# A graph network of four layers: 768 columns of its second adjacency sweep behind the attention sweep and at two levels

## Chip, core and metric

The kernel runs on one core of a Trainium2 chip, in float32. The time is what the device takes for one execution of the whole program, in microseconds (us). A core has a matrix engine (TensorE, PE in the profile; PEld is its weight loading), a vector engine (VectorE, DVE), a scalar engine (ScalarE, ACT) and GpSimd (POOL). SyncE (SP), ACT and POOL issue DMA transfers. Each engine works through its own list of instructions in order, and waits in front of one until what it needs is there.

## What is computed

`adj` is a sparse 2708 x 2708 matrix held dense, `x` has 2708 rows of 512 features. Four layers follow one another, each a residual and a layer normalisation:

```python
deg = maximum((adj != 0).sum(-1), 1)
# layer 0
inc = adj + mask / norm(mask)                     # mask = adj > 0, by row
x = LN(x + (inc @ x) / inc.sum(-1))
# layer 1
ts = adj @ x
gate_a, gate_b = sigmoid([ts, x] @ Wa.T + ba), sigmoid([ts, x] @ Wb.T + bb)
e = where(adj != 0, exp(-leaky_relu(x @ W_sa @ a_l + (x @ W_sa @ a_r).T)), 0)
x_a = (e / (e.sum(1) + 1e-5)) @ (x @ W_sa)
x_b = adj @ (x @ W_gcn) + b_gcn
x = LN(x + sigmoid(gate_a * x_a + gate_b * x_b))
# layer 2: p = adj @ p three times, out = x @ w0 + p1 @ w1 + p2 @ w2 + p3 @ w3
x = LN(x + out)
# layer 3
x = LN(x + relu(((adj + I) scaled by deg on both sides @ x + x) @ W_out + b_out))
```

So there are seven products of a 2708 x 2708 matrix with a 2708 x 512 one: one for layer 0, two for layer 1 (`adj @ x`, from which both the gates and x_b are made, and the attention product), three hops for layer 2 (the product by a weight is folded in after Horner, so that the innermost factor is x @ w3, called Y0) and one for layer 3.

## The kernel before

**Tiling.** The matrix is taken transposed (`adjT`), in four quarters of 1354 x 1354 (NH), called 11, 12, 21, 22. The inner dimension runs in ten tiles of 128 rows (KW) and 74 leftover rows (KR), which are done apart (`rest`). The free dimension, "columns" here, belongs to the rows of the result. X is held in SBUF as blocks B11, B12, B21, B22 with the sums T1 to T4, in groups A to D of three k tiles (B and D hold two each, and have a spare third part, `spare_part`, in which weights and score vectors are kept).

**One-level sweep** (`sweep`, line 374). A product is made from quarters by the scheme of Winograd, with seven products in place of eight, PLAIN giving their order. It takes its columns in ranges, RANGES on line 30: 384, 384, 256, 330. In a range each of the seven products has ten k tiles and two halves of the features, 140 matmuls. `load` brings the tiles of adjT on SP's queue; `comb` (line 400) makes the sums s1 to s4 of the quarters on DVE, ahead of the product that reads them. In the second sweep `comb` also stores each sum to DRAM (SD, shown as As), on POOL's queue, for the later sweeps.

**Two-level sweep** (`sweep2`, line 1181). The scheme is applied twice, 49 products in place of 64. RANGES2 (line 42) has two groups, 338 and 339 columns wide, each holding two such strips of each half. ORDER2 gives the order of the seven outer products. In each, `load` brings four strips of five k tiles (K2) from adjT or from the stored sums; `comb` (line 1212) makes inner sums of strips on DVE, `tsum` (line 1246) those of X; `step` (line 1267) multiplies; `leave` (line 1291) and `add` (line 1303) combine the outer products on DVE. The hops have a sixth k tile (ext), which multiplies X2 (the result of layer 1, stored transposed as X2T) by a weight, with its own quarter sums (`ext_loads`, `ext_sums`, SE).

**Stages.** `S = 28 s` gives stage s a place of 28 units. Work is put at a position by `at(pos, fn)`; the list is sorted by position, and a scheduler takes the order within each engine from it, freely from position 5 (START) on. A call with `hold=True` pins its instructions behind the one before on the same engine. Stages: S[0] layer 0, S[1] `adj @ x` of layer 1, S[2] the attention product, S[3] to S[5] the hops, S[6] layer 3. A one-level range has 7 units, a group of the two-level sweep 14.

**Around S[1].** `spread_v` (line 891) writes the four score vectors over the partitions. `score` (line 904) multiplies a tile of X1 by each of them on DVE, eight operations a tile of 128 rows, placed 0.95 units apart; `scores_end`, `score_rows`, `scores_over` turn them into `s_left`, `s_right` and `gate_x`. `tally` (line 965) counts the entries of a column tile by tile on DVE (`deg`). `done1` (line 996) makes the gates, and for the first three ranges x_b with the seven-product form (`row_sums`, `seven`, lines 624 and 638), for the last with `dense` (line 600). What it stores is XB.

**S[2].** `prep2` (line 1061) makes the attention weights of a tile: two ACT activations (lines 1066, 1067) and one DVE operation (line 1068), in place of the tile `a` of adjT. `done2` (line 1088) multiplies by W_sa, adds XB, applies the sigmoid and the layer normalisation (`layernorm`, line 553; its power is a POOL instruction on line 560), transposes X2 and makes Y0 with `dense`.

## Time and profile before

| | us |
|---|---|
| median of 3 runs | 2887.13 |
| their lowest and highest | 2880.56, 2888.68 |
| the profiled execution | 2883.33 |
| its span, first to last instruction | 2881.2 |
| PE busy in it | 2832.7 |
| DVE busy in it | 2195.9 |

The page adds up what each engine was busy with. The windows view does so for stretches of the span, in columns for PE, PEld, DVE, ACT and POOL, with the granted clock of PE, the mean busy share of the 16 DMA engines and GB/s. The timeline gives start, duration and name of merged records. The view of waits gives what an engine stood still for. A line of a group ends with its count, its busy time, the mean of one in ns, and the idle time before it with what ended it:

```profile
L1212 DVE TENSOR_TENSOR z<-z 128x339 f32<-128x339 f32 (+1 forms) x966 | 454.3, 503 | 12.5 <-PE accu L1267 3.2
L403 DVE TENSOR_TENSOR a<-a,a 128x384 f32<-128x384 f32 (+2 forms) x330 | 162.4, 510 | 23.1 <-PE accu L458 22.4
L965 DVE SCALAR_TENSOR_TENSOR deg<-a,deg 128x384 f32<-128x384 f32 (+2 forms) x152 | 75.2, 505 | 19.0 <-DMA a<-in_adjT 17.9
```

In the trace the second sweep starts at about 431 us, the attention sweep at about 830, the first hop at 1366, and layer 3 at 2482 us of the span.

### The profile page before, as it was taken

To read this page: it belongs to the slowest core of one execution; us is meant where nothing else is said; L and a number is where in the kernel's file an instruction comes from. 1 tells how busy PE (TensorE), PEld (TensorE's weight loads), DVE (VectorE), ACT (ScalarE), POOL (GpSimd) and SP (SyncE) were. 2 spreads that over 40 slices of the span, in tenths; PEclk is the share of its full clock that TensorE was granted. 3 is DMA by queue.
4 is the path that set the end of the run, shared out by engine and by line. 5 is a ranking of instruction groups with operands and counts; after the bars stand their busy time and mean duration, and the time that the engine had idled before them with its cause. 6 is when DMAs were issued, how large, how long until landed. Compare 5 with 4: busy or idle time off the path is not lost. (4 is left out here: it accounts for less than half of the span.)

```text
span 2881.2 us, 37482 instructions
## 1 busy us (share of the span) xinstructions
PE 2832.7 (98%) x10963; PEld 1870.3 (65%) x10963; DVE 2195.9 (76%) x5670; ACT 550.1 (19%) x1119; POOL 617.6 (21%) x1113
## 2 busy tenths in 40 slices
PE   7999999999999999999999999999999999999998
PEld 5655665657765656866666666666666666666665
DVE  6898798576736464654699787887878877799987
ACT  4544200111136444542100000000000100100001
POOL 0123223123320101122203123031230211501202
PEclk9999999999999999999999999999999999999999
DMA  7665466354544333565667767566675666754542
GB/s 229 193 212 179 133 204 218 124 181 143 183 140 130 117 113 98 151 198 151 195 205 236 213 192 246 166 201 208 187 250 168 181 197 182 230 174 145 175 142 92
DMA packets 368524, 510.04 MB, mean 177 GB/s; under 512 B 63424, under 2 KB 321700, under 8 KB 368320
## 3 DMA queue, kind: packets, MB, share of 16 engines
q1 hardware_dynamic: 302392, 370.56, 43.5%
q0 software_dynamic: 49344, 126.38, 13.1%
q10 hardware_dynamic: 16584, 10.71, 1.3%
q8 instruction: 87, 1.43, 0.2%
q14 instruction: 117, 0.96, 0.1%
HBM read 423.77 MB, written 83.65 MB: 176 GB/s over the span
## 5 line engine op out<-in xcount | busy, mean ns | idle before, releaser
L1212 DVE TENSOR_TENSOR z<-z 128x339 f32<-128x339 f32 (+1 forms) x966 | 454.3, 503 | 12.5 <-PE accu L1267 3.2
L1285 ACT COPY q<-accu 128x338 f32<-128x338 f32 (+1 forms) x84 | 34.6, 443 | 1003.3 <-PE accu L1267 806.0
L560 POOL TENSOR_TENSOR rstd<-rstd,neg_half 128x1 f32<-128x1 f32 (+3 forms) x91 | 59.3, 652 | 762.2 <-DVE rstd L559 516.6
L1267 PE MATMUL accc<-s,t 128*128 128x338 f32 (+1 forms) x644 | 198.1, 450 | 0.0
L1267 PE MATMUL accu<-z,t 128*128 128x338 f32 (+1 forms) x644 | 194.0, 448 | 1.5 <-DVE z L1212 1.5
L1267 PE MATMUL accd<-z,t 128*128 128x338 f32 (+1 forms) x644 | 193.9, 448 | 0.6 <-DVE q L1349 0.6
L1267 PE MATMUL accc<-z,t 128*128 128x338 f32 (+1 forms) x644 | 193.5, 448 | 0.5 <-ACT q L1285 0.5
L1400 POOL DMA_DIRECT2D Y<-y x192 | 105.1, 554 | 366.3 <-DVE y L1395 333.3
L403 DVE TENSOR_TENSOR a<-a,a 128x384 f32<-128x384 f32 (+2 forms) x330 | 162.4, 510 | 23.1 <-PE accu L458 22.4
L1267 PEld LDWEIGHTS accc<-s,t 128*128 128x128 f32 x644 | 120.9, 190 | 64.1 <-issue 7.5
L1267 PEld LDWEIGHTS accc<-z,t 128*128 128x128 f32 x644 | 122.0, 190 | 61.6 <-issue 1.0
L1267 PEld LDWEIGHTS accu<-z,t 128*128 128x128 f32 x644 | 121.7, 190 | 61.7 <-DVE z L1212 2.0
L1267 PEld LDWEIGHTS accd<-z,t 128*128 128x128 f32 x644 | 121.9, 190 | 60.5 <-DVE q L1349 1.5
L1212 DVE TENSOR_TENSOR s<-z 128x338 f32<-128x338 f32 (+1 forms) x322 | 149.7, 503 | 12.7 <-PE accc L1267 8.4
L1291 DVE TENSOR_TENSOR q<-q,accd 128x338 f32<-128x338 f32 (+1 forms) x112 | 56.0, 500 | 115.2 <-PE accd L1267 115.2
L1068 DVE SCALAR_TENSOR_TENSOR a<-a,e 128x384 f32<-128x384 f32 (+2 forms) x160 | 77.4, 507 | 49.8 <-ACT e L1067 49.5
L1066 ACT ACTIVATE e<-row,s_right 128x384 f32<-128x384 f32 (+5 forms) x176 | 96.3, 569 | 76.2 <-PE accc L458 20.4
L965 DVE SCALAR_TENSOR_TENSOR deg<-a,deg 128x384 f32<-128x384 f32 (+2 forms) x152 | 75.2, 505 | 19.0 <-DMA a<-in_adjT 17.9
L406 POOL DMA_DIRECT2D As<-a x120 | 64.9, 544 | 82.3 <-DVE a L403 80.3
L1067 ACT ACTIVATE e<-e 128x384 f32<-128x384 f32 (+5 forms) x176 | 79.3, 477 | 1.8
L606 PE MATMUL ps_d<-w,xT 128*128 128x512 f32 (+1 forms) x176 | 79.2, 593 | 0.4 <-ACT xT L597 0.4
L769 DVE SCALAR_TENSOR_TENSOR s<-a,row 128x384 f32<-128x384 f32 (+2 forms) x152 | 75.0, 505 | 6.0 <-ACT row L754 6.0
(683 smaller groups left out, 5869.0 us busy)
## 6 DMA issues: line engine op xcount, KB each, us to landing
z<-As SPq DMA_DIRECT2D x320, 169.5 KB
z<-As SPq DMA_DIRECT2D x320, 169.0 KB
a<-in_adjT SPq DMA_DIRECT2D x240, 192.0 KB
z<-in_adjT SPq DMA_DIRECT2D x240, 169.5 KB
z<-in_adjT SPq DMA_DIRECT2D x240, 169.0 KB
a<-in_adjT SPq DMA_DIRECT2D x120, 165.0 KB
a<-in_adjT SPq DMA_DIRECT2D x112, 128.0 KB
As<-a POOLq DMA_DIRECT2D x60, 192.0 KB, 4.2
```

The source lines that it names most:

```text
L403: nc.vector.tensor_tensor(A[r, dst, k][:, :n], A[r, a, k][:, :n], A[r, b, k][:, :n], op)
L406: nc.gpsimd.dma_start(out=SD[m][k * P : (k + 1) * P, R0 : R0 + n], in_=A[r, dst, k][:, :n])
L560: nc.gpsimd.tensor_tensor(rstd[:w, 1:2], rstd[:w, 0:1], neg_half[:w], ALU.pow)
L606: nc.tensor.matmul(o, lhs(c), r, start=c == 0 and n == 0, stop=c == DC - 1, skip_group_check=True)
L769: nc.vector.scalar_tensor_tensor(t[:w, :n], a[:w, :n], 0.0, row[R0, h][:w, :n], ALU.is_gt, ALU.mult)
L965: nc.vector.scalar_tensor_tensor(d[:w, :n], a[:w, :n], 0.0, d[:w, :n], ALU.not_equal, ALU.add)
L1066: nc.scalar.activation(e[:w, :n], row[R0, h][:w, :n], AF.Prelu, bias=s_right[:w, t : t + 1], alpha=0.01)
L1067: nc.scalar.activation(e[:w, :n], e[:w, :n], AF.Exp, scale=-1.0)
L1068: nc.vector.scalar_tensor_tensor(a[:w, :n], a[:w, :n], 0.0, e[:w, :n], ALU.not_equal, ALU.mult)
L1212: nc.vector.tensor_tensor(d[:, :n], Z[x + (k,)][:, :n], Z[y + (k,)][:, :n], op)
L1267: nc.tensor.matmul(B[home][:, :n], stat(v, k), a[:, :n], start=bool(start and k == 0), stop=k == nk - 1, skip_group_check=True)
L1400: nc.gpsimd.dma_start(out=rows[:, :, f * P : (f + 1) * P], in_=o[32 * f : 32 * (f + 1), : m * P].rearrange("p (b d) -> p b d", d=P))
```

## The change

The second sweep (S[1]) keeps only the columns from 768 on (RANGES_A) and takes 14 units in place of 28. Columns 0 to 767 are done in a new stage B at position 70, between the attention sweep and the first hop, as one group of the two-level sweep with strips of 384 columns (RANGES_B). For that the groups of all two-level sweeps become 293 and 384 wide.

The sums of quarters for those columns, which the sweep made on its way, are made in S[2] by a background task of its own: for each of two strips of 384 columns and each of ten k tiles four tiles are loaded on POOL's queue into six buffers (the four weight buffers `w_0` to `w_3` and two of the pool `nat`), counted (`back_tally`), summed (`back_sums`) and stored. The tallies and sums are held. The score sums of all tiles come within S[1]; those for the gates of columns below 768 come in S[2] with a second fetch of X1. `done2` leaves x_a of these columns, without gate, in XB. `doneB` makes gates, x_b with `dense`, X2 and Y0 for them; Y0 of the others follows in stage B from X2T. `W[3]` is loaded there. Positions of some loads in `next_x2` move with it.

```diff
-RANGES2 = [(0, 338), (676, 339)]
+RANGES_A = [(768, 256), (1024, 330)]
+RANGES_B = [(0, 384)]
+SPLIT = 768
+RANGES2 = [(SPLIT, 293), (0, 384)]
...
-    S = [28.0 * s for s in range(8)]
+    S = [0.0, 28.0, 42.0, 84.0, 112.0, 140.0, 168.0]
+    SB = 70.0
...
+    def score(t, w, got, js):
+        x1 = got.pop(t)
         junk = nat("vy")
-        for j in range(4):
+        for j in js:
             for e in range(2):
                 nc.vector.scalar_tensor_tensor(junk[:w, :HD], x1[:w, e * HD : (e + 1) * HD], 1.0, V[j, e][:w],
                                                ALU.mult, ALU.mult, accum_out=sc2[:w, t, e, j : j + 1])
...
+    for R0, n in RANGES_A + RANGES[:2]:
+        whole = R0 >= SPLIT
         for h in (1, 0):
-            for k in tiles_of(R0, n):
-                def go(t=h * KT + k):
-                    got1[t] = fetch(X1[t])
-
-                at(S[1] + 0.7 + 0.95 * i, go)
-                at(S[1] + 1.1 + 0.95 * i, lambda t=h * KT + k, w=wt(k): score(t, w, got1))
+            ts = tiles_of(R0, n)
+            for k in ts:
+                p = S[1] + 0.6 + 0.45 * i
+                at(p, lambda t=h * KT + k: get_x1(t))
+                at(p + 0.35, lambda t=h * KT + k, w=wt(k), js=range(4 if whole else 2): score(t, w, got1, js))
                 i += 1
-            at(S[1] + 1.12 + 0.95 * (i - 1), lambda R0=R0, h=h, ts=tiles_of(R0, n): scores_end(R0, h, ts))
-            at(S[1] + 1.6 + 0.95 * (i - 1), lambda R0=R0, h=h, ts=tiles_of(R0, n): score_rows(R0, h, ts))
-    at(S[1] + 1.13 + 0.95 * (i - 1), scores_over)
+            at(p + 0.36, lambda a=(h * KT + ts[0], len(ts), False): scores_end(*a))
+            if whole:
+                at(p + 0.36, lambda a=(h * KT + ts[0], len(ts), True): scores_end(*a))
+            at(p + 1.0, lambda R0=R0, h=h, ts=ts: score_rows(R0, h, ts), True)
+    at(p + 0.37, scores_over)
+    for i, (h, k) in enumerate((h, k) for h in (1, 0) for k in range(SPLIT // P)):
+        p = S[2] + 1.6 + 1.7 * i
+        at(p, lambda t=h * KT + k: get_x1(t))
+        at(p + 0.4, lambda t=h * KT + k: score(t, P, got1, (2, 3)), True)
+        if k == SPLIT // P - 1:
+            at(p + 0.41, lambda a=(h * KT, k + 1, True): scores_end(*a))
...
-    sweep(S[1], RANGES, extra=extra1, done=done1, late=0.85, save=True)
+    sweep(S[1], RANGES_A, extra=extra1, done=done1, late=0.85, save=True)
...
+    def back_tile(c):
+
+        i = back["i"] = (back.get("i", -1) + 1) % 6
+        t = feat.tile([P, D], F32, name="bk", tag=f"w_{i}") if i < 4 else nat("bk")
+        back["next"][c] = t
+        return t
...
+    QUARTERS = ((1, 0), (1, 1), (0, 0), (0, 1))
+    BW = 384
+
+    def back_load(i0, k, half):
+        if not half:
+            back["next"] = {}
+        for hi, hj in QUARTERS[2:] if half else QUARTERS[:2]:
+            j0, c0 = hj * NH + k * P, hi * NH + i0
+            nc.gpsimd.dma_start(out=back_tile((hi, hj))[:, :BW], in_=adjT[j0 : j0 + P, c0 : c0 + BW])
+        if half:
+            back["t"] = back["next"]
...
+    def back_tally(i0, ws):
+        for h in range(2):
+            for j, w in enumerate(ws):
+                a = back["t"][h, j]
+                if (i0, h) not in deg:
+                    deg[i0, h] = d = tmp("deg")
+                    nc.vector.tensor_scalar(d[:w, :BW], a[:w, :BW], 0.0, None, ALU.not_equal)
+                else:
+                    d = deg[i0, h]
+                    nc.vector.scalar_tensor_tensor(d[:w, :BW], a[:w, :BW], 0.0, d[:w, :BW], ALU.not_equal, ALU.add)
...
+    def back_sums(i0, k):
+        a21, a22, a11, a12 = (back["t"][q][:, :BW] for q in QUARTERS)
+        for m, o, a, b, op in (("s1", a22, a21, a22, ALU.add), ("s3", a21, a11, a21, ALU.subtract),
+                               ("s2", a11, a22, a11, ALU.subtract), ("s4", a12, a12, a11, ALU.subtract)):
+            nc.vector.tensor_tensor(o, a, b, op)
+            nc.gpsimd.dma_start(out=SD[m][k * P : (k + 1) * P, i0 : i0 + BW], in_=o)
...
+    widths = [n + 60 for _, n in RANGES]
+    ends = [7 * sum(widths[:i]) for i in range(5)]
+
+    def place_at(t):
+
+        i = max(i for i in range(4) if ends[i] <= t)
+        return S[2] + 7 * i + (t - ends[i]) / widths[i]
+
+    t0, dt = 1.2 * widths[0], (26.2 / 28 * ends[4] - 1.2 * widths[0]) / 21
+    at_t = lambda j, fn, hold=False: at(place_at(t0 + dt * j), fn, hold)
+    j = 0
+    for i0 in range(0, SPLIT, BW):
+        for k in range(KW):
+            at_t(j - 0.4, lambda i0=i0, k=k: back_load(i0, k, 0))
+            at_t(j + 0.02, lambda i0=i0, k=k: back_load(i0, k, 1))
+            at_t(j + 0.6, lambda i0=i0: back_tally(i0, (P, P)), True)
+            at_t(j + 0.61, lambda i0=i0, k=k: back_sums(i0, k), True)
+            j += 1
+        at_t(j, lambda i0=i0: back_rest_load(i0))
+        at_t(j + 0.6, lambda i0=i0: back_tally(i0, (KA, 32)), True)
+        for h in range(2):
+            at_t(j + 1.2, lambda a=(i0, h): back_end(*a), True)
+            at_t(j + 1.5, lambda a=(i0, h): back_rows(*a), True)
+        j += 1
...
+                if not whole:
+                    y = nat("xa")
+                    nc.scalar.mul(y[:w], px[:w], rd[t][:w])
+                    move(nc.gpsimd, XB[t], y[:w])
+                    return
...
+    def startB():
+        W[1] = [spare_part(s, g) for s in ("T1", "T2", "T3", "T4") for g in "BD"]
+        for i, t in enumerate(W[1]):
+            nc.scalar.dma_start(out=t, in_=w_gcn[i // 2 * P : (i // 2 + 1) * P, i % 2 * HD : (i % 2 + 1) * HD])
+
+    def startB3():
+        W[3] = load_w(w_hop[3])
+
+    def restB():
+        lo, hi = X1[KT - 1], X1[2 * KT - 1]
+        for e in range(2):
+            s = REST_HOMES[e][1]
+            group(s, "R")
+            nc.gpsimd.dma_start(out=groups[s, "R"][0], in_=copies(hi[KA - KR :, e * HD : (e + 1) * HD], 4))
+
+    at(SB - 0.2, startB3)
+    at(SB + 1.0, restB)
+    at(SB + 2.5, startB)
...
+    def y0_last(t, w, r0):
+        g, (i0, m) = next((g, r) for g, r in enumerate(RANGES2) if r[0] <= r0 and r0 + w <= r[0] + 2 * r[1])
+        xT = pool.tile([P, DC, P], F32, name="xT", tag="xT", bufs=2)
+        nc.sync.dma_start(out=xT[:, :, :w], in_=X2T[g, t // KT][:, r0 - i0 : r0 - i0 + w].rearrange("(c p) i -> p c i", p=P))
+        y0_rows(xT, w, t)
+
+    for i, (R0, h, k) in enumerate((R0, h, k) for R0, n in RANGES_A for h in (1, 0) for k in tiles_of(R0, n)):
+        at(SB + 1.6 + 0.75 * i, lambda t=h * KT + k, w=wt(k), r0=k * P: y0_last(t, w, r0))
...
+    def doneB(p0, dp, g, i0, n, h, cc, tiles):
+        Z = {}
+        t0, m = h * KT + i0 // P, len(tiles)
+
+        def gates(s):
+            pg = bank("pg")
+            for c in range(DC):
+                nc.tensor.matmul(pg[32 * c : 32 * c + 32, :n], wab_pad[:, c, :], cc(s, c)[:, :n], start=True, stop=True)
+            Z[s] = ring_tile("zg")
+            nc.scalar.copy(Z[s][:, :n], pg[:, :n])
...
+            def b(s=s, lo=lo, t=t, got=got):
+                px = dense(lambda c: cc(s, c)[:, lo : lo + P], W[1], P)
+                got["y"] = y = nat("y")
+                nc.vector.tensor_tensor(y, px, vec[1], ALU.add)
+                nc.scalar.mul(y, y, gate[:, t, 1:2])
+                nc.vector.scalar_tensor_tensor(y, got["xa"], gate[:, t, 0:1], y, ALU.mult, ALU.add)
...
+    sweep2(SB, 0, doneB, ranges=RANGES_B)
...
-        for g, p in enumerate((S[2] + 19.3 + 1.1 * i, S[3] + 6.6 + 1.3 * i)):
+        for g, p in enumerate((SB + 4.3 + 1.6 * i, S[3] + 6.6 + 1.3 * i)):
```

## The prediction

> **What bounds the kernel now.** I read the totals of the page first, then the waits of PE, then busy time in stretches.
>
> ```profile
> PE 2832.7 (98%) x10963; PEld 1870.3 (65%) x10963; DVE 2195.9 (76%) x5670; ACT 550.1 (19%) x1119; POOL 617.6 (21%) x1113
> ```
> ```profile
> core: us from the first to the last instruction, mean granted TensorE clock
> core 0: 2881.2 us, clock 0.998
> ```
>
> A PE that is 98% busy may still be waiting inside its instructions, so I checked the pace in the timeline of PE:
>
> ```profile
> 2511.86 3.00 PE L1267 MATMUL accd<-z,t 128*128 128x338 f32 x10
> 2514.70 3.00 PE L1267 MATMUL accu<-z,t 128*128 128x338 f32 x10
> ...
> 466.38 4.03 PE L458 MATMUL accd<-a,T1A 128*128 128x384 f32 x12
> 470.25 2.74 PE L458 MATMUL accd<-a,T1B 128*128 128x384 f32 x8
> ```
>
> Ten records of 338 columns take 2.84 us (2511.86 to 2514.70), 284.0 ns each; twelve of 384 take 3.87 us, 322.5 ns. That is 0.836 ns a column, and it holds through long runs. So PE is the bound by columns. Each matmul of the code is two such records: the three k tiles and two column halves that use T1A are six matmuls and x12 here. PE's idle time is 48.5 us. About 23 us lie in the first 144 us and 7.5 in the last 73, which the change leaves alone. Most of the other 18 is in two places, both with a busy DVE:
>
> ```profile
> core 0: us, PE busy (x) PEld busy (x) DVE busy (x) ACT busy (x) POOL busy (x), PEclk, DMA share, GB/s
> 395.00:515.00 120.00, 114.28 (x427) 70.76 (x427) 102.14 (x332) 5.60 (x16) 41.65 (x76) 1.00 0.70 228
> 827.00:1366.00 539.00, 538.58 (x2007) 351.63 (x2004) 295.12 (x713) 257.29 (x483) 80.58 (x137) 1.00 0.45 134
> 1529.00:1705.00 176.00, 176.00 (x633) 115.97 (x632) 147.16 (x355) 4.61 (x12) 28.03 (x52) 1.00 0.68 203
> 2481.60:2662.20 180.60, 174.76 (x663) 116.51 (x662) 162.62 (x413) 17.43 (x32) 41.75 (x74) 1.00 0.59 176
> ```
>
> Row one is the start of the second sweep: DVE 85% busy, PE idle 5.7 us. Row two is the attention sweep: DVE 55%, PE full. Row three is a two-level half-sweep with a sixth k tile: DVE 84%, PE full. Row four is the first half of the last sweep, five k tiles: DVE 90%, PE idle 5.8 us. The reader should see that a stretch is safe at 84% DVE and loses about 3% of its time at 90%.
>
> [...] The trace starts such operations 0.42 and 0.47 us apart (2519.09 to 2519.51; 0.47 between 384-column ones). So DVE carries about 0.07 us an instruction that does not shrink with the tile. [...] with the attention sweep at a DMA share of 0.45 I charge no bandwidth.
>
> **The change, part by part.** Columns 0 to 767 leave the one-level second sweep.
>
> (1) Matmuls. Two ranges of 140 products of 384 columns go: 280 x 2 x 0.3225 = 180.6 us. Sweep B does them with 7 x 7 x 5 = 245: 158.0 us. Gain 22.6. The leftover rows (KR) cost the same on both sides.
>
> (2) Weight products. The seven-product form for these twelve tiles goes, 84 products of 256 columns; B multiplies plainly, 96 of them. At 0.2157 us a record (256 columns, same pace) that is +12 x 2 x 0.2157 = +5.2 us.
>
> (3) Retiling of the later sweeps, 338/339 to 293/384: the columns are the same sum (677), the products too, so 0 on PE. The weight products of Y0, the transposes and the gates move and are as many as before. Sum on PE: **-17.4 us**.
>
> (4) DVE, second sweep. Before, 22 tiles of score sums (8 operations each) were spread over 21 of 28 units; now all come within 9.5 of 14 units, 128 operations, beside the tallies and sums of the 256- and 330-column ranges, whose matmuls are shorter. Taking the operations in the order in which the two programs hold them, from the transposes that spread the score vectors on, at (N/0.96 + 70) ns: beside the first 120 us of matmuls DVE has 81 us of work before and 119 us after. No slack is left to recover what the start loses. The start itself loses more: the first product used to cover the wait for the last layernorm's B11 tiles (waits of 2.1 and 1.0 us) with 16 products of 384 columns, and has 16 of 256, 16 x 2 x 0.107 = 3.4 us less cover. Bounds: +2 (the queue catches up in the next range) to +10 (119 us at row one's 85% would need 140 us; half of that appears). I take **+7**.
>
> (5) The background task in the attention sweep. Twenty steps of four tallies and four sums, 160 x 0.47 = 75 us, leftovers 4, the gate scores of twelve tiles 12 x 4 x 0.42 = 20: +99 us on DVE. Layernorms of twelve tiles (about 2 us each) and the sums for X2T go to B: -31. PE loses 22 x 8 x 0.43 = 76 us of Y0 products and 7 of transposes to B. DVE: (295 + 68) / 456 = 80%, under the safe 84% on average. But the tallies are pinned behind the DVE instruction before them, and a DVE that waits for their tile makes the masks `a` of the attention behind it wait, for which PE waits. The tiles come on POOL's queue: the load waits until the store of the tile's last sum has landed.
>
> ```profile
> cl<-in_adjT POOLq DMA_DIRECT2D x40, 192.0 KB, 4.8
> As<-a POOLq DMA_DIRECT2D x60, 192.0 KB, 4.2
> ```
>
> So 4.2 + 4.8 = 9 us from the last sum to the next use, and POOL's queue stands meanwhile (its stores of XB behind it). In the program's order about six of the twenty steps have under 5 us of matmuls between the last load and its tally, the others 8 or more. Six waits of about 5 us, each with a lead of DVE over PE of the order of a few us (the attention masks are placed 0.7 of a unit ahead of use). Bounds: 0 (the lead covers all) to 40 (every step costs 2 us). I take **+6**.
>
> (6) Sweep B: DVE has about 150 us of work beside 263 us of matmuls, ACT and DMA are light: nothing. Its two seams, with weights reloaded into the tiles that the background used, I put at **+2** (-2 to +10); the Y0 products of ten tiles are filler there.
>
> (7) Two-level sweeps at 293 columns. Per record PE drops by 37.5 ns, per operation DVE by 47 ns, but PE has two records per product. First half of the last sweep: PE 174.8 - 2 x (245 + 16) x 0.0375 = 155.2; DVE 162.6 - 208 x 0.047 = 152.8 (its 8 sums of X tiles per product do not shrink). That is 98% of PE's time where 90% lost 5.8 us. At DVE's present 90% the half takes 170 us, idle 14.6; at 95%, 161, idle 5.7. I take an idle of 13, **+7**. The second half relaxes from 85% and can give back a little of its own. In the three hop sweeps a half at 293 has by the same sums (row three: 176 - 620 x 0.0375 = 152.8 of PE, 147.2 - 246 x 0.047 = 135.6 of DVE) 89% in place of 84, and the first one starts on a burst of ext operations: **+3** (0 to 8).
>
> Sum: -17.4 + 7 + 6 + 2 + 7 + 3 = **+7.6 us**. Against the profiled run (2883.33 us, span 2881.2 and 2.1 around it) 2891. The median of the three runs is 3.8 higher; on it, 2887.1 + 7.6, about **2895**.
>
> **Rivals.** (A) The forecast: the matmuls saved are paid back as DVE waits. 2895, own range 2885 to 2905, 0.47.
>
> (B) DVE's queue absorbs it. For it: the row at 84% without idle, and waits of PE on DVE that are short (a z tile of L1212: 5 waits, longest 0.5 us). Against: 90% already loses. Extra idle then is about 5 us: 2887 - 17 + 5 = 2875. Chance 0.21.
>
> (C) The background's pinned tallies hold up DVE at every step. For it: loads behind stores in one queue, eight operations in a block (3.8 us). Against: DVE at 55% there before, PE idle 0.4 in 539 us. Price: 20 x 2 us = 40 in place of 6, so 2895 + 34 = 2929. It decides once wait plus block (about 9 us) exceeds DVE's lead over PE in most steps. Chance 0.24.
>
> (D) 84% is all that DVE reaches in the hop sweeps: 135.6 / 0.84 = 161 us in place of 152.8, three times +8.6, in place of the 3: 2895 + 23 = 2918. Against: row four gets 90%. Chance 0.08.
>
> **How the numbers follow.** What the measurement can tell from no change is about 0.3%, 8.7 us: 2878.5 to 2895.8. B is faster (0.19 of its 0.21); A splits about evenly at its middle, 0.26 within and 0.21 slower; C and D are slower but for 0.02. Faster 0.20, same 0.29, slower 0.51. The range takes in B's middle and C's: 2872 to 2930.
>
> **What would show it.** PE's records should fall short of before by about 17 us of busy time at an unchanged pace; PE's idle between the first 144 us and the end should rise from about 18 to over 40 us. Step 4: waits of PE on deg, s_left and a tiles in the first 130 us of the second sweep, DVE over 95%. Step 5: DVE waiting for `bk` from DMA in the attention sweep, PE waiting behind it. Step 7: PE idle of 10 us or more in the first half of the last sweep. If idle outside the start stays under 25 us, B holds and I am wrong on DVE; if the attention sweep alone idles over 25 us, C does.

## The result, and the profile after

The changed kernel takes 2911.3 us (median of 4 runs, 2907.78 to 2913.9), the kernel before 2886.91 in runs on the same chip: a ratio of 1.0088, with a 95% interval of 1.0069 to 1.0107. It is 24 us slower where +8 was forecast. The profiled execution took 2907.78 us with a span of 2906.0, 24.8 more than the span of before. First its totals, then busy time in stretches:

```profile
PE 2830.1 (97%) x10917; PEld 1861.5 (64%) x10917; DVE 2272.2 (78%) x5811; ACT 549.1 (19%) x1113; POOL 636.5 (22%) x1153
```
```profile
core 0: us, PE busy (x) PEld busy (x) DVE busy (x) ACT busy (x) POOL busy (x), PEclk, DMA share, GB/s
393.00:513.00 120.00, 109.27 (x495) 83.81 (x494) 105.80 (x425) 7.92 (x24) 47.04 (x86) 0.94 0.63 187
630.60:1075.40 444.80, 436.02 (x1692) 299.27 (x1691) 328.88 (x862) 204.33 (x403) 123.73 (x225) 1.00 0.61 181
1075.40:1345.40 270.00, 266.14 (x893) 155.08 (x892) 158.63 (x346) 35.38 (x62) 57.38 (x101) 1.00 0.64 193
1762.00:1919.30 157.30, 157.11 (x654) 118.43 (x653) 141.19 (x356) 7.60 (x20) 33.50 (x63) 1.00 0.70 206
2496.40:2665.40 169.00, 158.69 (x664) 114.33 (x663) 149.04 (x401) 16.80 (x32) 31.47 (x57) 1.00 0.57 168
```

The rows are the start of the second sweep, the attention sweep, sweep B, a hop sweep's narrow half, and the last sweep's narrow half. PE's busy time fell by 2.6 us only, although 46 records fewer ran, and its idle time rose from 48.5 to 75.9 us. The reader should see two things. The attention sweep, which had 0.4 us of idle, has 8.8 (444.8 less 436.0, row two); and in the first row the granted clock (the column PEclk) is 0.94 where it was 1.00.

Busy time hides what a slower clock and short waits inside records cost: from 439.20 to 443.44 us of the changed kernel PE is busy for all of the 4.24 us at a granted clock of 0.50, and a record of 338 columns lasts about 448 ns where the next one starts after 284. So I compared each stretch with its pace: every PE record at the start-to-start distance of its width, summed. Twelve records in a row give 322.5 ns each at 384 columns in both kernels, 284.2 and 285.0 at 338 and 339 before, 246.7 at 293 after: N x 0.8333 + 2.5 ns for all of them. Records of 32 rows or 32 columns, most of which start four together (in the kernel before 424 of 452 and 56 of 64, each four within 20 ns), count a quarter; the few kinds under 100 columns count their median. What a stretch takes beyond that is lost time, whatever its form. The stretches are cut at the first product of each sweep, which puts the start of the attention sweep of the kernel before at 865.0 us, not at 827 as in the prediction's row two. In us, with three experiments told below:

| stretch | before | changed | e4 | e9 | e12 |
|---|---|---|---|---|---|
| first sweep | 49.6 | 47.5 | 47.3 | 45.6 | 49.3 |
| second sweep | 17.9 | 22.2 | 18.1 | 24.0 | 22.6 |
| attention sweep | 4.5 | 15.6 | 4.2 | 14.2 | 4.6 |
| sweep B | - | 7.4 | - | 4.6 | 5.1 |
| first hop sweep, first half | 3.5 | 11.6 | 6.8 | 12.6 | 13.5 |
| the other five hop halves | 10.0 | 13.3 | 11.7 | 12.2 | 13.7 |
| last sweep | 12.9 | 20.4 | 18.7 | 19.9 | 20.7 |
| lost in all | 98.3 | 138.0 | 106.7 | 133.1 | 129.4 |
| PE at its pace | 2772.2 | 2754.8 | 2772.2 | 2754.8 | 2754.8 |

So the change saves 17.4 us of matmuls and loses 39.7 more; with 2.5 us more after PE's last record that is the 24.8.

### The profile page after: what moved, and what is told of

Read it like the earlier page. It is cut to its first block, busy times and chain, and to the rows that moved or that the text cites. A ratio compares the mean times of both kernels' runs of the same rounds, so it can differ in the third digit from the quotient of the medians.

```text
span 2906.0 us, 37814 instructions
## 1 busy us (share of the span) xinstructions
PE 2830.1 (97%) x10917; PEld 1861.5 (64%) x10917; DVE 2272.2 (78%) x5811; ACT 549.1 (19%) x1113; POOL 636.5 (22%) x1153
## 3 DMA queue, kind: packets, MB, share of 16 engines
q1 hardware_dynamic: 317776, 387.52, 45.6%
## 4 chain that ended last, share of the span: by engine, by line
PE 80%; DVE 10%; DMA 4%; issue 3%; POOL 2%; SPq 1%; ACT 1%; POOLq 0%; DVEq 0%; ACTq 0%
PE accd L1388 13%; PE accu L1388 13%; PE accc L1388 13%; PE ps_d L610 7%; PE acca L1388 6%; PE accd L462 5%; PE accc L462 5%; PE accu L462 5%; PE accr L1459 3%; PE acca L462 2%; PE ps L649 2%; DVE z L1333 1%; PE accr L1463 1%; PE accd L471 1%; POOL rstd L564 1%
## 5 line engine op out<-in xcount | busy, mean ns | idle before, releaser
L1333 DVE TENSOR_TENSOR z<-z 128x384 f32<-128x384 f32 (+1 forms) x1071 | 507.9, 507 | 22.3 <-PE accu L1388 8.1
L1388 PE MATMUL accc<-s,t 128*128 128x384 f32 (+1 forms) x714 | 224.7, 455 | 0.6 <-DVE rstd L563 0.6
L1388 PE MATMUL accd<-z,t 128*128 128x384 f32 (+1 forms) x714 | 220.0, 453 | 3.8 <-DVE z L1333 2.1
L1388 PE MATMUL accu<-z,t 128*128 128x384 f32 (+1 forms) x714 | 219.0, 453 | 2.8 <-DVE z L1333 2.2
L1388 PE MATMUL accc<-z,t 128*128 128x384 f32 (+1 forms) x714 | 218.4, 452 | 3.0 <-issue 1.9
L564 POOL TENSOR_TENSOR rstd<-rstd,neg_half 128x1 f32<-128x1 f32 (+2 forms) x91 | 58.3, 641 | 658.9 <-DVE rstd L563 389.4
L1412 DVE TENSOR_TENSOR q<-q,accd 128x384 f32<-128x384 f32 (+1 forms) x126 | 63.8, 506 | 137.4 <-PE accd L1388 136.8
L1333 DVE TENSOR_TENSOR s<-z 128x384 f32<-128x384 f32 (+1 forms) x357 | 167.8, 507 | 1.0 <-DMA Es<-a 0.4
L1470 DVE TENSOR_TENSOR q<-q,accr 128x384 f32<-128x384 f32 (+1 forms) x144 | 65.0, 504 | 33.4 <-PE accr L1463 33.1
L1412 DVE TENSOR_TENSOR q<-q,accu 128x384 f32<-128x384 f32 (+1 forms) x162 | 78.4, 517 | 7.5 <-ACT q L1406 6.3
L1412 DVE TENSOR_TENSOR q<-q,accc 128x384 f32<-128x384 f32 (+1 forms) x96 | 49.3, 514 | 42.4 <-PE accc L1388 42.2
```

Of the source, the lines that this page charges most:

```text
L564: nc.gpsimd.tensor_tensor(rstd[:w, 1:2], rstd[:w, 0:1], neg_half[:w], ALU.pow)
L1333: nc.vector.tensor_tensor(d[:, :n], Z[x + (k,)][:, :n], Z[y + (k,)][:, :n], op)
L1388: nc.tensor.matmul(B[home][:, :n], stat(v, k), a[:, :n], start=bool(start and k == 0), stop=k == nk - 1, skip_group_check=True)
L1412: nc.vector.tensor_tensor(d[:, :n], s_[:, :n], B[home][:, :n], ALU.add)
L1470: nc.vector.tensor_tensor(d[:, :n], d[:, :n], ps[r][:, :n], ALU.add)
```

## Experiments

All ran beside the kernel before; ratios are to it. Lengths of a sweep are from the one profiled execution of each kernel. The attention sweep takes 443.4 to 446.7 us in four of them that leave it as it is (the changed kernel, e2, e8, e9), and the second sweep 201.3 to 206.2 us in seven, so a smaller difference says little. Of the names in the views, `C` and `P1c` are finished combinations of the seven products, `ld` is a tile of features on its way through a layernorm, `rstd` its scale, `bk` a tile of the background, and `z` an inner sum of the two-level sweep.

**e1: the layernorm's last step back on DVE.**

```diff
-        layernorm([(x1, 0, D)], x1, w, True)
+        layernorm([(x1, 0, D)], x1, w)
```

> The changed kernel with the last step of the layernorm of X2 back on DVE, as in the kernel before (one DVE operation in place of a DVE operation and an ACT one). Theory: the three waits of PE on ld from ACT in the attention sweep (5.0 us) come from the route over POOL, DVE and a busy ACT; they shrink under 2 us, PE's idle in the attention sweep falls by 3 to 5 us and the time to about 2905. Rival: the wait is the layernorm's chain itself (POOL's power step, DVE's queue of tallies), whichever engine ends it: the waits on ld stay at about 5 us and the time at 2911 within 3.

2909.09 us, ratio 1.0075 (1.0060 to 1.0091). PE's waits on `ld` fell from 5.0 us to 2.3, but those on `C` and `P1c` rose from 3.8 to 4.5; the attention sweep took 442.4 us in place of 444.8, which is 1.0 under the lowest of its spread. A small part of the effect may be there, the rest of the loss is elsewhere. In the same run the second sweep, which the edit does not touch, took 206.2 us in place of 201.3: the stall at its start varies by some us from run to run, and stretches must be compared, not totals.

**e2: tallies later at the start of the second sweep.**

```diff
+            if R0 == RANGES_A[0][0] and ij == "11":
+                p = 0.3
```

> The changed kernel with the first twenty tallies of the second sweep (quarter 11 of the first range) placed 0.9 of a unit later, behind the copies P1c. Theory: DVE no longer waits for adjacency tiles ahead of the copies that PE needs, the wait of PE on P1c (5.66 us) goes, and with it the halved clock after it (about 5 us more): second sweep 8 to 10 us shorter, 2902. Rival: DVE has too much work in that sweep (119 us beside 120 us of matmuls), the tallies moved are missed later, PE waits for deg, s_left or a instead, and the sweep is shorter by under 3 us: 2909 to 2912.

2910.81 us, 1.0081 (1.0064 to 1.0099); second sweep 205.7 us. The 5.7 us wait on `P1c` went, and PE waited 3.5 us for the layernorm behind it, 3.5 for `rdeg`. The rival holds.

**e3: no DVE work in the background.**

```diff
-            nc.vector.tensor_tensor(o, a, b, op)
...
-            at_t(j + 0.6, lambda i0=i0: back_tally(i0, (P, P)), True)
```

> The changed kernel without the DVE work of the background task in the attention sweep: its 80 tallies and 80 quarters' sums are left out (the loads and stores stay; the entry counts of these 768 columns and the sums for sweep B are wrong). Theory: this work costs the attention sweep about 6 us (the waits on P1c and C, 3.8 us, and a clock lowered after them), so the sweep goes from 444.8 to about 439 us and the time to 2905. Rival 1: the background is the whole of the sweep's 11 us over the pace: 434 us, 2900. Rival 2: it costs nothing, the waits on ld are all: 444, 2911.

2909.28 us, 1.0082 (1.0065 to 1.0099). DVE's busy time in the attention sweep fell by 65 us, to 264 of 444, and the sweep by 1.0, which is inside its spread. Rival 2 is nearest: the background's work on DVE, the +99 us that step (5) priced first, is not what the sweep pays for.

**e4: the narrow tiling alone, in the kernel before.**

```diff
-RANGES2 = [(0, 338), (676, 339)]
+RANGES2 = [(0, 293), (586, 384)]
```

> The kernel before with one line changed: the later sweeps' ranges are (0, 293) and (586, 384) in place of (0, 338) and (676, 339), so that their first half is as narrow as in the changed kernel, and nothing else of the change is there. Theory: the narrow half costs by itself, about 7 us in the last sweep and 3 in the hop sweeps: 2897, with PE idle of 13 us in the first half of the last sweep. Rival 1: what the later sweeps lost in the changed kernel came with the order of loads and with work moved into them, and the tiling alone costs nothing: 2887. Rival 2: narrow halves are the whole of the loss of 16.5 us that the later sweeps show: 2903 or more.

2893.78 us (9 runs), ratio 1.0026 (1.0016 to 1.0035): +7.5 us where I had said 10. In the table 10.8 us more are lost in the last three stretches (3.3, 1.7 and 5.8), and 2.3 fewer in the first sweep. PE's idle in the last sweep's first half is 7.6 us where I had said 13, but with it goes time lost inside records. The theory holds, at three quarters of its size.

**e5: rows of the attention earlier in SP's queue.**

```diff
-        at(pb - 1.6, lambda: rows(0))
-        at(pb - 1.0, lambda: rows(1))
+        at(pb - (3.0 if r else 1.6), lambda: rows(0))
+        at(pb - (2.4 if r else 1.0), lambda: rows(1))
```

> The changed kernel with the loads of the rows for the attention's second to fourth range placed 1.4 units earlier, ahead of the fetches of X1 and XB in SP's queue. Theory: those fetches wait for buffers of the one ring of six that the background's tiles now share, the rows stand behind them (ACT waited 15.6 us for a row until 936.95), ACT's exponentials and the layernorms on ACT come late, and PE then waits for ld and P1c (7.2 us and a halved clock). With the rows early ACT's wait falls under 5 us, PE's waits in the attention sweep from 8.8 us to under 5, the sweep from 444.8 to 438 to 441 us, the time to about 2905. Rival: the layernorm's own chain over DVE, POOL and ACT is late whatever the rows do: waits on ld stay near 5 us, the sweep within 2 us of 444.8.

2913.3 us, 1.0091 (1.0073 to 1.0109). ACT's 15.6 us wait for a row is gone, the waits on `ld` fell from 5.0 to 1.9 us, and those on `C` rose from 1.6 to 5.8; the sweep took 447.5 us. Neither was right: the rows were late, but were not what PE paid for.

**e6: the background with four tiles in place of six.**

```diff
-        i = back["i"] = (back.get("i", -1) + 1) % 6
-        t = feat.tile([P, D], F32, name="bk", tag=f"w_{i}") if i < 4 else nat("bk")
+        i = back["i"] = (back.get("i", -1) + 1) % 4
+        t = feat.tile([P, D], F32, name="bk", tag=f"w_{i}")
...
-            at_t(j - 0.4, lambda i0=i0, k=k: back_load(i0, k, 0))
+            at_t(j - 0.3, lambda i0=i0, k=k: back_load(i0, k, 0))
```

> The changed kernel with the background's tiles in four weight tiles alone, none in the ring of six that fetches, scores and outputs share; its first pair of loads is issued 0.1 of a step later so that its buffers can come free. Theory (the ring is what blocks SP): fetches no longer wait for the background's stores, the row comes early, PE's waits in the attention sweep fall from 8.8 to under 6 us. Rival (what the prediction priced): with four tiles each load waits for the store of the step before, DVE's held tallies wait for bk for more than 25 us instead of 9, the masks behind them come late, and the sweep is longer than 447 us.

2946.68 us, 1.0210 (1.0193 to 1.0226); the sweep took 481.1 us. The view of waits in its attention sweep (us in total, times, longest):

```profile
DVE deg L1112 <- DMA bk<-in_adjT: 45.9, 18, 5.6
...
PE ps_d L610 <- DVE C L523: 24.9, 4, 9.0
```

The first line is the held tally waiting for its tile at nearly every step, the second is PE waiting behind it. This is the prediction's case (C), at +36 us, made real by two buffers fewer (and by first loads 0.1 of a step later). With six tiles DVE waited 8.9 us on `bk`, five times.

**e7: the wide range first in the second sweep.**

```diff
-RANGES_A = [(768, 256), (1024, 330)]
+RANGES_A = [(1024, 330), (768, 256)]
```

> The changed kernel with the two ranges of the second sweep in the other order, 330 columns first and 256 second. Theory: what PE lacks at the sweep's start is cover, since the products before the first wait are 256 columns wide; with 330 the 16 products in front of the last layernorm's tiles take 2 us more (32 records x 0.062 us), the waits on P1c and ld of the first 15 us (8.3 to 11.5 us in the changed kernel and its variants; 2.1 and 2.0 before) shrink by 2 us or more and the halved clock after them is shorter: second sweep 3 to 5 us shorter. Rival: DVE waits for an adjacency tile that comes when a ring slot is freed, PE waits as long whatever the width: 201 to 206 us as before.

2916.84 us, 1.0099 (1.0081 to 1.0117). The second sweep took 207.7 us, with one wait of 8.9 us for the last layernorm. Two us of cover bought nothing: the rival holds, though the sweep is 1.7 us over the 206 that it named.

**e8: the tail of sweep B drawn together.**

```diff
-            p = p0 + 0.4 + 0.28 * i
+            p = p0 + 0.35 + 0.2 * i
...
-            at(p + 0.7, e)
-            at(p + 0.85, y0)
+            at(p + 0.6, e)
+            at(p + 0.72, y0)
```

and the first Y0 products of B at `SB + 2.4` in place of `SB + 1.6`.

> The changed kernel with the tail of sweep B drawn together (the six tiles of its second half 0.2 of a unit apart in place of 0.28, transposes and Y0 products 0.1 earlier) and its first Y0 products 0.8 of a unit later. Theory: PE's 3.0 us of waits on z in the first hop sweep come from a chain on POOL's queue (each load of a B11 tile waits there until the store of Y0 ahead of it has landed, 2 to 6 us, six times), and the 2.1 us at the start of B from a Y0 tile fetched before it is stored; both go, and B plus the first hop half is 4 to 6 us shorter (482.4 to about 477). Rival: the layernorms of the six tiles, closer together, wait for each other on DVE, POOL and ACT, and PE waits in sweep B's end instead: within 2 us.

2908.41 us, 1.0077 (1.0061 to 1.0093); B and the half after it took 482.1 us in place of 482.4. PE's waits in the two stretches:

```profile
PE pg L1527 <- DVE q L1412: 2.9, 1, 2.9
...
PE accu L1388 <- DVE z L1333: 0.2, 1, 0.2
```

The 2.2 us on `z` and the 2.1 at B's start went as the theory had it, and DVE's wait for `B11C` fell from 4.8 to 1.1 us. But 2.9 us on `pg` came and the wait of line 1459 for leftover rows grew from 0.3 to 1.5, and by the pace the two stretches lost 18.7 us in place of 19.0: the rival's sum, if not in its place.

**e9: DVE's order at the start of the second sweep by hand.**

```diff
+        early = (0.9, 1.1) if R0 == RANGES_A[0][0] else (-0.6, 0.05)
+        for ij, p in (("11", early[0]), ("21", early[1]), ("22", 1.05), ("12", 3.6)):
...
+                at(pb + p + 0.8 * k / KT, lambda ij=ij, k=k: tally(int(ij[0]) - 1, (ij, k)), ij[1] == "1" and R0 == RANGES_A[0][0])
...
+                at(pb + cw["s3"] + f + (0.3 - 0.3 * k / nk if r == 0 and save else 0),
+                   lambda k=k, comb=comb: comb("s3", "11", "21", ALU.subtract, k), r == 0 and save)
```

> The changed kernel with DVE's order at the start of the second sweep put right by hand: the tallies of the first range's quarters 11 and 21 and the differences s3 are held behind the copies P1c and the last layernorms of the sweep before, in place of between them. Theory: PE's waits at the start (5.3 to 11.5 us in the changed kernel and seven variants, with 10 us of halved clock) come from a tally that stands between the copies and the layernorm on DVE and waits for an adjacency tile (5 to 7 us), and from nothing else; they fall to 2 or 3 us as in the kernel before, no 10 us of half clock follows, the second sweep takes 192 to 197 us in place of 201 to 206 and the time is about 2902. Rival: DVE is short of time in this sweep (119 us of work beside 120 us of matmuls), and what is put off is missed later: waits on s, deg, s_left or rdeg grow by as much and the sweep stays over 199 us.

2905.83 us, 1.0076 (1.0059 to 1.0093). What it was to mend, in the timeline of the changed kernel (start, length, what ran, and the idle time before it with its releaser):

```profile
431.62 0.42 DVE L986 SCALAR_TENSOR_TENSOR deg<-a,deg 128x256 f32<-128x256 f32 x1
431.95 0.49 DVE L523 TENSOR_TENSOR P1c<-P1c,acca 128x330 f32<-128x330 f32 x1
437.59 0.42 DVE L986 SCALAR_TENSOR_TENSOR deg<-a,deg 128x256 f32<-128x256 f32 x1 [5.15 <-DMA a<-in_adjT]
437.93 0.49 DVE L523 TENSOR_TENSOR P1c<-P1c,acca 128x330 f32<-128x330 f32 x1
...
438.48 0.48 PE L593 MATMUL ps_n<-ident,P1c 128*128 128x128 f32 x1 [5.66 <-DVE P1c L523]
```

A tally stands between the two halves of `P1c` and waits for its adjacency tile; PE waits for the second half. With the tallies held back these waits are gone, and the view of waits of that sweep in e9 reads:

```profile
PE accd L463 <- DVE a L407: 6.5, 4, 3.9
PE ps_r L933 <- DVE s_left L927: 2.7, 1, 2.7
PE accc L463 <- DVE s L407: 2.3, 3, 0.9
```

As much as before, spread over the next 60 us: what was put off is missed there. The sweep took 203.1 us, so the rival holds. In its first 120 us DVE now waits 0.7 us for adjacency tiles in place of 9.7 and is busy for 110.4, so late tiles alone do not explain the length. That the DVE work beside too few matmuls does is the likeliest reading; no run took work out of DVE in this sweep.

**e10: the background as copies in DRAM.**

```diff
-            at_t(j - 0.4, lambda i0=i0, k=k: back_load(i0, k, 0))
-            at_t(j + 0.02, lambda i0=i0, k=k: back_load(i0, k, 1))
-            at_t(j + 0.6, lambda i0=i0: back_tally(i0, (P, P)), True)
-            at_t(j + 0.61, lambda i0=i0, k=k: back_sums(i0, k), True)
+            at_t(j + 0.61, lambda i0=i0, k=k: back_copy(i0, k))
...
+    def back_copy(i0, k):
+        for m, (hi, hj) in zip(("s1", "s3", "s2", "s4"), QUARTERS):
+            j0, c0 = hj * NH + k * P, hi * NH + i0
+            nc.gpsimd.dma_start(out=SD[m][k * P : (k + 1) * P, i0 : i0 + BW], in_=adjT[j0 : j0 + P, c0 : c0 + BW])
```

> The changed kernel with the background task replaced by a stand-in that moves as many bytes at the same places: four copies a step from the adjacency straight into the arrays of the sums, on POOL's queue, with no tile in SBUF, no tally and no sum on DVE (the sums for sweep B and the counts of these 768 columns are wrong). Theory: the attention sweep's 11 us over the pace come from the background's tiles, which share a ring of six with all fetches and stand in the queues of POOL and SP, not from its DVE work (whose removal alone gave 1 us): the sweep falls from 444.8 to 434 to 437 us, time about 2902. Rival: it is what left the sweep (the Y0 products that covered the layernorm's chain) and the layernorm's last step on ACT: waits on ld stay at 4 to 5 us and the sweep at 441 or more.

2936.16 us, 1.0182 (1.0167 to 1.0198), but not for the reason asked about. The copies need no tile, and all 80 were moved ahead into the first sweep, which grew from 426.1 to 466.4 us. The attention sweep, now without any background, took 432.9 us with no idle at all. Of tiles and traffic this run cannot say which.

**e11: the wide half first, in the kernel before.**

```diff
-RANGES2 = [(0, 338), (676, 339)]
+RANGES2 = [(0, 384), (768, 293)]
```

> The kernel before with one line changed: the later sweeps' ranges are (0, 384) and (768, 293), so the wide half comes first and the narrow one second. Theory (a half loses time as its DVE work approaches its PE work, whichever half it is): the first half of the last sweep, 90% DVE before, relaxes to 88% and its idle falls from 5.8 to 3 to 5 us; the second goes from 85% to about 92% and loses 5; the hop sweeps' second halves are spared the ext operations and lose nothing. Together near nothing: 2886 to 2890. Rival 1: only the first half's ext burst makes a narrow half costly, so that the wide one first is a gain: 2880 to 2883. Rival 2: the narrow half costs the same 8 us wherever it stands: 2894.

2881.48 us (12 runs), ratio 0.9992 (0.9984 to 1.0001): no loss, and no gain that can be told. Of the three forecasts rival 1 named this time, but not for its reason: the last sweep, which has no ext operations, loses 12.3 us here and 18.7 in e4. The last sweep's halves in the kernel before (its second half), in e4 (first) and in e11 (both), in the view by stretches:

```profile
2662.20:2873.80 211.60, 210.84 (x779) 138.91 (x777) 184.33 (x473) 16.25 (x24) 33.61 (x60) 1.00 0.47 140
```
```profile
2484.30:2651.30 167.00, 159.42 (x664) 115.82 (x663) 148.19 (x400) 16.59 (x32) 42.52 (x78) 0.99 0.58 171
```
```profile
2476.50:2672.60 196.10, 194.73 (x664) 117.70 (x663) 175.25 (x414) 18.16 (x32) 29.86 (x52) 1.00 0.58 179
2672.60:2868.00 195.40, 192.37 (x779) 137.25 (x777) 170.34 (x462) 16.06 (x24) 25.47 (x46) 1.00 0.45 133
```

DVE is busy for 87, 89, 89 and 87% of them, and PE's idle is 0.8, 7.6, 1.4 and 3.0 us. The mean share of DVE does not tell a safe half from a losing one. In these runs a narrow half is dear where it comes first.

**e12: as e10, with the copies held in place.**

```diff
-            at_t(j + 0.61, lambda i0=i0, k=k: back_copy(i0, k))
+            at_t(j + 0.61, lambda i0=i0, k=k: back_copy(i0, k), True)
```

> As e10, but the copies are held to their places in the order of POOL's queue, so that they run in the attention sweep and not ahead of it (the sums for sweep B and the counts of these 768 columns are wrong). With that the sweep has the background's bytes (twice 192 KB a copy, 80 copies) without its tiles, its DVE work and its waits for DVE and for landed stores. Theory: the tiles and the waits are the cost, not the bandwidth: the sweep stays at 432 to 436 us (444.8 in the changed kernel, 432.9 without any background traffic), and the whole at about 2896. Rival: the traffic itself makes the rows and adjacency tiles of the attention late: 440 us or more.

2901.69 us, 1.0052 (1.0036 to 1.0069). The attention sweep in e3 and in e12:

```profile
634.00:1077.80 443.80, 435.43 (x1692) 299.66 (x1691) 264.23 (x706) 198.82 (x401) 122.90 (x225) 1.00 0.59 182
```
```profile
632.90:1066.60 433.70, 433.15 (x1691) 298.93 (x1690) 264.19 (x706) 198.48 (x401) 79.25 (x145) 1.00 0.53 149
```

DVE has the same work in both (264.2 us); e3 keeps the background's tiles in SBUF with their waits, e12 has copies, without tiles and with few of the waits. The first loses 8.4 us of idle, the second 0.6. So the tiles with their waits cost the sweep 10 us (443.8 to 433.7), and 11 with the DVE work. The theory holds for them, though its total of 2896 was 6 us too low. What of the tiles costs it is not separated: from e3 to e12 POOL's waits for landed transfers of the background fall from 64.3 to 12.0 us, the background's tiles leave the ring of six, and POOL has half as many of its transfers to issue (busy 79.3 us in place of 122.9).

For the traffic the theory holds in part. From e10, with none, to e12 and e3 the sweep moves 113, 149 and 182 GB/s at a DMA share of 0.39, 0.53 and 0.59: a copy adds about half of what a load and a store add. That half cost under 1 us (432.9 to 433.7); the rest was not tried by itself.

One way in which they cost it shows in the timeline of the changed kernel, at one layernorm of X2:

```profile
984.19 0.15 DVE L563 TENSOR_SCALAR rstd<-mv 128x1 f32<-128x1 f32 x1
...
985.61 0.54 POOL L1091 DMA_DIRECT2D bk<-in_adjT  x1 [2.00 <-DMA As<-bk]
986.41 0.54 POOL L1091 DMA_DIRECT2D bk<-in_adjT  x1 [0.26 <-issue]
986.94 0.55 POOL L152 DMA_DIRECT2D X<-ld  x1
987.50 0.57 POOL L564 TENSOR_TENSOR rstd<-rstd,neg_half 128x1 f32<-128x1 f32 x1
...
988.10 0.16 DVE L566 SCALAR_TENSOR_TENSOR rstd<-mv,rstd 128x1 f32<-128x1 f32 x1 [3.76 <-POOL rstd L564]
...
988.30 0.81 ACT L569 ACTIVATE ld<-ld,rstd 128x512 f32<-128x512 f32 x1 [5.87 <-DVE rstd L566]
...
989.16 0.66 PE L599 MATMUL ps_t<-ident,ld 128*128 128x128 f32 x4 [2.19 <-ACT ld L569]
```

DVE has the variance ready at 984.34. The power step is POOL's, and stands there behind loads of background tiles, one of which waits 2.0 us for the store of an older sum to land. So it runs at 987.50; DVE stood still for 3.76 us, ACT and PE follow. The load writes over a tile that the store reads, POOL waits those 2.0 us ahead of issuing it, and all that POOL has queued behind pays for it: the power step starts 3.16 us after the variance. In e12 the longest wait of DVE for POOL's `rstd` in the sweep is 0.9 us, in e3 7.2.

## Why the prediction was right or wrong

It said slower, and 2911 lies in its range; the middle, 2895, was 16 us too low. Some of that is luck. Slower had a chance of 0.51, the range was drawn wide enough for rivals (B's middle and C's), and the forecast's own range, 2885 to 2905, misses. By its steps, profile against profile:

| step | on record | measured |
|---|---|---|
| (1) to (3) PE | -17.4 | -17.4 |
| (4) second sweep | +7 | +4.3 |
| (5) background | +6 | +11.1 |
| (6) sweep B and seams | +2 | +12.2 |
| (7) narrow halves | +10 | +14.2 |
| first sweep, and after PE's end | 0 | -2.1, +2.5 |
| sum | +7.6 | +24.8 |

- (1) to (3) came out to the tenth: the pace did not change, and e4 shows that the tiling alone adds nothing to PE at its pace (2772.2 in both). PE's busy time did not show it (2.6 us less), since waits and a lower clock inside records count as busy.
- (4) was right in size, a little high. Its price of a DVE operation, which (5) and (7) share, holds in the traces: where TENSOR_TENSOR records of one width follow without idle time, the median from start to start is 421 ns at 338 columns before, 374 at 293 and 469 at 384 after, so 1.04 ns a column and 68. In seven runs with the same second sweep and an undisturbed first one the loss is 4.3 to 9.2 us over before, 5.9 on average. Crowded DVE work is the likeliest reason: e7 gave PE more cover and e9 a better order, and neither helped. That is not shown as an experiment without the work would show it, and the sign on record, DVE over 95%, did not come (105.8 of the 120 us in row one, 88%). That the waits fell on `P1c`, `deg` and `s_right` was not foreseen in full, nor the clock.
- (5) had a mechanism that the trace shows, a load that waits on POOL for a landed store while POOL's queue stands, and was 5 us low. It named the held tallies as the victim, which with six tiles make DVE wait 8.9 us on `bk`, and the stores of XB behind the loads. It left out the layernorm's power step, which is on POOL too: 5.0 of PE's 8.8 us of idle in the sweep are waits for that layernorm. It also left out that the change moves the layernorm's last step to ACT, one engine more in the chain (e1: 2.4 us of the sweep at most). The DVE work, on which its text spent most, costs no more than the spread (e3: 1 us).
- (6) is the step that failed, by 10.2 us of the 17; its own bounds were -2 to +10. B itself, put at nothing, loses 7.4 us, and the first hop half 4.8 more than in e4, which has the tiling alone. In ten runs with this code the step comes to 9.0 to 13.4 us, 11.0 on average. About half of it is idle time: PE waits 3.9 us in B, 2.1 of them for a tile of X2T fetched for Y0 and 1.8 for a transposed tile from ACT, and 3.8 us in the hop half, where e4 has 1.6. The step overlooked that X2T and Y0 go through DRAM here, on POOL's queue. Timeline of the changed kernel, at the start of the first hop sweep:

```profile
1421.32 0.54 POOL L152 DMA_DIRECT2D B11B<-Y  x1 [2.98 <-DMA Y<-y]
1421.85 0.54 POOL L152 DMA_DIRECT2D T3B<-Y  x1
1422.45 0.55 POOL L152 DMA_DIRECT2D Y<-y  x1
1428.80 0.54 POOL L152 DMA_DIRECT2D B11C<-Y  x1 [5.80 <-DMA Y<-y]
...
1431.51 0.56 DVE L1367 TENSOR_TENSOR t<-B11C,B11A 128x384 f32<-128x384 f32 x1 [4.79 <-DMA B11C<-Y]
...
1448.51 0.76 PE L1388 MATMUL accu<-z,t 128*128 128x293 f32 x2 [2.22 <-DVE z L1333]
```

  Each tile of the new X waits for a store of Y0 to land, DVE waits for the tile, then works off its backlog, and PE waits 17 us after the cause. This chain is in the trace, but that it sets the price is not shown: e8 took the waits on `z` and at B's start away, and the two stretches lost as much (18.7 in place of 19.0). What the step put at nothing is known with its size; how it divides among causes stays open.
- (7) was right in size at first sight: e4 shows +7.5 us by the clock for the tiling alone, and 10.8 in these halves. The 3.4 us more that they lose in the changed kernel were not traced. Its reason was not right. It rested on DVE's mean share, and e11 has the same shares without the loss. What in a first half makes the narrow tile dear was not separated.
- Case (B), that DVE absorbs it, is out: between the first 144 us and the last 73 PE idles 42.3 us in place of 17.4, and the sign on record for (B) was under 25. Case (C) is the mechanism of e6, not of the change with six tiles. Case (D) is out: the hop half with DVE at 90% (fourth stretch above) has 0.2 us of idle.

No version tried beats both kernels: e11 cannot be told from the kernel before, and e9 stays 0.76% above it; so does e12 by 0.52%, though it leaves out the sums and the counts of 768 columns.

## What to carry to other kernels

When background work was put into a stretch with a half idle engine here, its instructions mattered less than its buffers and queues (e3 against e12): list everything issued on the queue where its loads wait for its own stores, small arithmetic steps included. Where several chains are near their limits, mending one wait by order alone (e2, e5, e8, e9) moved it to the next; of all edits only taking the tiles with their waits out (e10, e12) shortened a stretch clearly. And a cut into unequal halves should be tried in both orders: here (0, 384) first cost nothing and 293 first 0.26%.

## What the runs showed of the hardware

Some waits of PE cost more than their length here. In the clock records of the changed kernel's trace the granted TensorE clock is 0.5 for 10.24 us from 434.0 us on, 1.2 us after the start of the wait of 5.66 us, for 3.41 us from 471.5, 1.0 after the end of a wait of 2.0, and for 3.41 us from 990.4, 1.2 after the end of one of 2.2; the kernel before has 6.83 us from 90.8, in the first sweep. Matmuls then start half as often (256 columns every 427 ns in place of 216, from 439 to 444 us in the changed kernel). In the 14 profiled executions, between 420 and 2860 us, all 12 waits over 4.5 us had such a stretch of 6.83 or 10.24 us, 21 of the 22 over 3 us had one, and 20 of the 38 between 2 and 3 us (17 of the 35 that have no longer wait within 12 us). The mean clock of the whole execution is 0.998 in the kernel before, e4 and e11, 0.995 in the changed kernel and 0.989 in e6, with waits up to 9.0 us. The first 50 us of the second sweep, before and after:

```profile
429.00:480.00 51.00, 45.87 (x165) 27.88 (x164) 42.72 (x129) 4.13 (x12) 22.45 (x41) 1.00 0.73 234
```
```profile
429.00:480.00 51.00, 40.27 (x180) 33.86 (x179) 41.52 (x172) 4.56 (x15) 21.35 (x40) 0.87 0.62 186
```

The kernel before has waits of 2.0 and 2.1 us there and no drop; the changed one has 5.66 us and a clock of 0.87. Its three drops of 10.24, 3.41 and 3.41 us from the second sweep on take at most half of 17.1 us, 8.5 of the 39.7 more that are lost (less where PE was waiting anyway).
